# Sending each token to its own expert alone in a two-layer fp32 transformer kernel

## The chip, the cores and the metric

The kernel runs on one core of a Trainium2 chip. The metric is the time on the device in microseconds (us), as the median of three runs. A core has five engines that run side by side, each through its own instructions in order: PE multiplies matrices (PEld loads its stationary operand), DVE is the vector engine, ACT the engine of activation functions, POOL a general-purpose engine, and SP issues transfers. DMA queues carry data between the main memory and the on-chip memories (SBUF; PSUM, into which PE writes).

## The reference

2048 tokens (two sequences of 1024) of width 128 pass four blocks, all in fp32: a retention layer with eight heads, a causal latent attention with 16 heads of width 8, a mixture of experts, and a full attention with 16 heads; a projection with ternary weights ends it. Layer norms stand between. The change touches the mixture of experts:

```python
def moe(x, gate_w, gate_b, W1, b1, W2, b2):
    logits = x @ gate_w.T + gate_b
    top = jnp.argmax(logits, axis=-1)
    onehot = jax.nn.one_hot(top, N_EXPERTS, dtype=x.dtype)       # N_EXPERTS = 4
    h = jax.nn.relu(jnp.einsum('btd,ehd->bteh', x, W1) + b1)     # W1: 4 x 512 x 128
    y = jnp.einsum('bteh,edh->bted', h, W2) + b2                 # W2: 4 x 128 x 512
    return jnp.einsum('bted,bte->btd', y, onehot)
...
x = x + mla_attention(rmsnorm(x, norm1_w), ...)
x = x + moe(rmsnorm(x, norm2_w), gate_w, gate_b, W1, b1, W2, b2)
```

Each token uses the output of one expert, that with the largest logit; the reference computes all four and masks three.

## The kernel before

The retention layer comes first and ends at about 290 us. Then both attentions run as one chain of 224 items, through a loop of ticks. An item is one tile of 128 keys by up to 512 queries for a group of four heads. In each tick `chain_tick` issues, for one item, four score matmuls (`sc`) and the maxima of their rows on DVE (`parts`); for the item 11 ticks back four transposed score matmuls (`sct`) and their exponentials on ACT (`es`); for the item 12 back four matmuls with the values (`acc`), which ACT evicts into `part` and POOL adds to `oT`. `part` is one buffer. In the diagonal tiles of the causal attention POOL also zeroes part of `es` (`bar`). After a group's last score its maxima go by PE, ACT and a small DMA on SP's queue (`qT<-m_rows`) into the queries, three ticks or more before `sct` needs them. All matmul outputs take turns in eight PSUM banks (`slot`). The causal attention fills items 0 to 95, the full one 96 to 223; a group of the full one has eight items, the first of which ACT evicts straight into `oT`.

Everything else runs beside this chain, as jobs cut into stages by `yield`. `side_work` runs at the head of a tick; of each of two lists of jobs, heavy and light, it steps the first one whose tick has come, and the number yielded is how many ticks the next stage has to wait. A job that is due is run to its end.

The heavy list holds the four experts jobs, one for each block of 512 tokens (2 sequences x 2 blocks). Such a job projects the attention's output, norms it (`rmsnorm_T`, which leaves the tokens as rows in `xn` and as columns in `xnT`), computes the gate and its one-hot `oh` on DVE, and then has 16 stages, four to an expert: two with two `first` each, two with two `second` each:

```python
for e in range(NE):
    hT = scratch("e_hT", "hT", (P, NF, BT))
    for i in range(0, NF, 2):
        first(e, i, hT)
        first(e, i + 1, hT)
        bias_2(e) if i else None
        yield 1
    for i in range(0, NC, 2):
        second(e, i, hT)
        second(e, i + 1, hT)
        yield 1
```

`first` is one matmul over 512 tokens (`ph`) and a relu on DVE or ACT; `second` is four accumulating matmuls with 128 tokens (`pmoe`), which DVE multiplies by `oh` and adds to `moe_acc`. `bias_2` adds the second bias on POOL. Then come the layer norm's moments and its application. The weights of all experts are loaded once, by two transfers of 1 MB on SP's queue at tick 12. The jobs' expert stages lie in ticks 37 to 52, 69 to 84, 94 to 109 and 119 to 134.

Of the kernel before, what the change touches and what calls it, by code (L numbers as in the profile page):

```python
# [14 lines left out]
P = 128  # L15
# [8 lines left out]
NE, FF = 4, 512  # L24
NF = FF // P
NEG = -1.0e9
NH = NG * GH
# [33 lines left out]
def block_kernel(  # L61
# [34 lines left out]
    for e in range(NE):  # L96
        nc.gpsimd.memset(rank[:, e : e + 1], float(NE - e))

    def dims(j):
# [58 lines left out]
    def slot(name):  # L158
        return banks[0](name)
# [23 lines left out]
    def transposed(src, name):  # L183

        tp = slot(name)
        for c in range(NC):
            nc.tensor.transpose(tp[:, c * P : (c + 1) * P], src[:, c, :], ident)  # L187
        return tp
# [23 lines left out]
    def scratch(tag, name, shape=(P, NC, P)):  # L212
        return scratch_of[0].tile(list(shape), F32, tag=tag, name=name)

    def rmsnorm_T(src, weight, got, lane=""):
# [9 lines left out]
        yield 2  # L225
        tp = transposed(xn, "xn_ps")
        got["xnT"] = scratch(lane + "xnT", "xnT", (P, BT))
        nc.scalar.activation(got["xnT"], tp, AF.Identity, scale=weight)
# [675 lines left out]
    late = ctx.enter_context(tc.tile_pool(name="late", bufs=1, reuse_waits="tile"))  # L904
    for i, name in enumerate(("w1", "w2")):
        at, n = M_W[name]
        mw[name] = late.tile([P, n], F32, name=f"m_{name}")

    def load_experts():
        for name in ("w1", "w2"):  # L910
            at, n = M_W[name]
            nc.sync.dma_start(out=mw[name], in_=m_w[:, at : at + n])

# [12 lines left out]
    def project(src, w, name, got, tag):  # L926
# [5 lines left out]
        got["py"] = by_tile(oT, w, f"{name}_ps")  # L932

    def experts(b, k):

        got = {}
# [4 lines left out]
        yield from rmsnorm_T(xa, col("norm2"), got, "e_")  # L941
        xnT = got["xnT"]
        pg = by_tile(xnT, mw["gate"], "pgate")
# [17 lines left out]
        nc.gpsimd.tensor_tensor(acc, x1[b][k], xa, ALU.add)  # L961
        yield 1

        def first(e, f, hT):
            ph = slot("ph")
            at = e * FF + f * P
            mm(ph, mw["w1"][:, at : at + P], xnT)
            bias = col("b1", e * NF + f)
            if f % 2:
                nc.vector.tensor_scalar(hT[:, f, :], ph, bias, 0.0, ALU.add, ALU.max)  # L970
            else:
                nc.scalar.activation(hT[:, f, :], ph, AF.Relu, bias=bias)

        def second(e, c, hT):
            py = slot("pmoe")
            for f in range(NF):
                at = (e * NF + f) * P
                mm(
                    py[:, :P], hT[:, f, c * P : (c + 1) * P], mw["w2"][:, at : at + P],
                    start=f == 0, stop=f == NF - 1,  # L980
                )
            nc.vector.scalar_tensor_tensor(  # L982
                acc[:, c, :], py[:, :P], oh[:, c, e : e + 1], acc[:, c, :], ALU.mult, ALU.add
            )

# [7 lines left out]

        for e in range(NE):
            hT = scratch("e_hT", "hT", (P, NF, BT))
            for i in range(0, NF, 2):
                first(e, i, hT)
                first(e, i + 1, hT)
                bias_2(e) if i else None
                yield 1  # L1000
            for i in range(0, NC, 2):
                second(e, i, hT)
                second(e, i + 1, hT)
                yield 1
        mv, r = stats(tiles(acc))
# [76 lines left out]
    def setup():  # L1082
        load_experts()
        yield from ternary()

    class Job:
# [3 lines left out]
        def step(self, tick):  # L1090
            try:
                self.at = max(self.at, tick) + next(self.stages)
            except StopIteration:
                self.done = True


    light = [
# [4 lines left out]
    ]  # L1102
    heavy = []
    for b in range(B):
# [161 lines left out]
```

## Time and profile before

| | us |
|---|---|
| median of three runs | 1192.27 (1191.64 to 1195.5) |
| the profiled execution's own time | 1191.54 |
| its span, first to last instruction | 1189.8 |
| PE busy / share of the span | 1102.6 / 93% |
| DVE busy / share | 825.9 / 69% |
| ACT busy / share | 710.4 / 60% |
| POOL busy / share | 479.8 / 40% |
| granted TensorE clock, mean | 0.975 |

Times below are from the one profiled execution. A group of the page is one line's instructions of one kind on one engine, with how often, how long in all and how long each; behind the bar stands the idle time of the engine before them and what ended it. An fp32 matmul shows as two PE records. The chain is followed back from the last instruction to what released each step, so its shares name what set the end. A line of a stretch gives the busy us of each engine in it, then the granted clock, the DMA share and GB/s. Line 82 is the helper that issues most matmuls, so tiles tell them apart.

### The profile page before, as it was taken

What the parts mean: (1) busy time and instruction counts of PE and PEld (TensorE: products, weight loads), DVE (VectorE), ACT (ScalarE), POOL (GpSimd) and SP (SyncE); (2) the same over time, 40 slices, a digit from 0 to 9 for tenths busy, and PEclk for the clock granted to TensorE, in tenths of its full rate; (3) what the DMA queues carried; (4) which work ended last, traced back from release to release, by engine and by line L of the source; (5) the groups of instructions that cost most, each with busy time, mean ns of one, the idle gap of its engine ahead of it and who ended that gap; (6) DMA issues with size and microseconds to landing.
All of it is one profiled execution on the core that took longest, in us unless ns stands there. A gap on an engine that the chain in (4) does not pass through costs nothing.

```text
span 1189.8 us, 22189 instructions
## 1 busy us (share of the span) xinstructions
PE 1102.6 (93%) x8554; PEld 604.3 (51%) x8554; DVE 825.9 (69%) x1822; ACT 710.4 (60%) x1439; POOL 479.8 (40%) x491
## 2 busy tenths in 40 slices
PE   6999999979889999999999999999989989998993
PEld 5888888755444554554444444444333333333322
DVE  4666766757766667676666677667788888888812
ACT  2465544432666556655565557556768867886891
POOL 4466445411656434443353334423333333323342
PEclk9999999986999999999999999999999999999996
DMA  5511112101000000100010001000100000000000
GB/s 187 164 37 45 41 41 45 28 10 73 10 11 19 1 2 1 21 3 1 2 19 1 1 4 18 2 1 1 19 10 2 1 2 10 1 2 10 1 1 9
DMA packets 14840, 25.56 MB, mean 21 GB/s; under 512 B 2960, under 2 KB 8400, under 8 KB 14352
## 3 DMA queue, kind: packets, MB, share of 16 engines
q1 hardware_dynamic: 14080, 22.30, 7.7%
q8 instruction: 67, 1.10, 0.4%
q0 software_dynamic: 224, 1.05, 0.2%
q10 hardware_dynamic: 432, 0.81, 0.2%
q14 instruction: 37, 0.30, 0.1%
HBM read 10.13 MB, written 1.05 MB: 9 GB/s over the span
## 4 chain that ended last, share of the span: by engine, by line
PE 72%; DVE 17%; POOL 4%; issue 3%; ACT 2%; DMA 1%; SPq 0%; POOLq 0%; DVEq 0%; ACTq 0%
PE sc L82 17%; PE acc L82 15%; PE sct L82 12%; PE pmoe L82 5%; PE ph L82 5%; DVE parts L353 5%; DVE spare L348 2%; PE py L82 2%; PE pv L82 2%; PE pr L82 2%; PE pout L714 1%; PE o_ps L187 1%; PE pg L82 1%; DVE x L205 1%; ACT es L397 1%
## 5 line engine op out<-in xcount | busy, mean ns | idle before, releaser
L397 ACT ACTIVATE es<-sct 128x512 f32<-128x512 f32 (+3 forms) x896 | 426.9, 558 | 218.6 <-PE sct L82 169.0
L353 DVE TENSOR_REDUCE parts<-sc 128x1 f32<-128x512 f32 x640 | 396.9, 682 | 94.4 <-PE sct L82 69.0
L82 PE MATMUL sc<-kT,qT 32*128 32x512 f32 (+3 forms) x1792 | 428.4, 584 | 5.5 <-DVE parts L348 2.7
L82 PE MATMUL sct<-qT,kT 32*128 32x512 f32 (+3 forms) x1792 | 410.6, 578 | 1.4 <-DMA qT<-m_rows 1.1
L423 POOL TENSOR_TENSOR oT<-oT,part 128x512 f32<-128x512 f32 (+3 forms) x192 | 217.5, 1133 | 392.3 <-ACT part L422 388.0
L82 PE MATMUL acc<-es,v_aug 128*32 128x512 f32 (+3 forms) x1792 | 221.6, 558 | 40.6 <-DVE parts L353 29.0
L82 PEld LDWEIGHTS sc<-kT,qT 32*128 32x128 f32 x1792 | 171.7, 189 | 145.2 <-DVE parts L353 73.9
L82 PEld LDWEIGHTS sct<-qT,kT 32*128 32x128 f32 x1792 | 179.1, 184 | 46.0 <-issue 23.3
L348 DVE CUSTOM_DVE_ANT_0 spare<-sc,causal 128x512 f32<-128x512 f32 (+3 forms) x256 | 125.4, 490 | 48.2 <-PE sc L82 12.8
L82 PEld LDWEIGHTS acc<-es,v_aug 128*32 128x32 f32 x1792 | 37.8, 108 | 196.0 <-DVE parts L353 112.5
L422 ACT COPY part<-acc 128x512 f32<-128x512 f32 (+3 forms) x192 | 105.7, 550 | 42.4 <-PE acc L82 36.3
L405 POOL TENSOR_SCALAR_AFFINE_SELECT es<-es 128x512 f32<-128x512 f32 x64 | 40.8, 637 | 118.5 <-ACT es L397 118.5
L771 ACT ACTIVATE og<-pt,cols_sb 128x128 f32<-128x128 f32 x128 | 46.5, 468 | 53.1 <-PE pt L763 53.1
L82 PEld LDWEIGHTS pmoe<-m_w,hT 128*128 128x128 f32 x512 | 59.6, 192 | 16.2 <-DVE parts L353 8.8
L82 PE MATMUL pmoe<-m_w,hT 128*128 128x128 f32 x512 | 65.0, 280 | 0.6 <-DVE parts L348 0.2
L82 PE MATMUL ph<-xnT,m_w 128*128 128x512 f32 x128 | 62.4, 610 | 0.0
L118 POOL TENSOR_TENSOR rstd<-rstd,nhalf 128x4 f32<-128x4 f32 (+1 forms) x44 | 54.7, 1244 | 3.6
L970 DVE TENSOR_SCALAR hT<-ph,cols_sb 128x512 f32<-128x512 f32 x32 | 24.0, 750 | 35.2 <-PE ph L82 35.2
L645 POOL TENSOR_TENSOR swap<-swap,r_cs 128x1024 f32<-128x1024 f32 x16 | 38.7, 2417 | 20.7 <-DMA swap<-plain 20.7
L982 DVE SCALAR_TENSOR_TENSOR moe_acc<-pmoe,oh,moe_acc 128x128 f32<-128x128 f32 x64 | 22.4, 350 | 35.2 <-PE pmoe L82 34.8
L668 ACT COPY v<-pv 128x1024 f32<-128x1024 f32 x16 | 16.2, 1012 | 43.8 <-PE pv L82 43.8
L82 PEld LDWEIGHTS ph<-xnT,m_w 128*128 128x128 f32 x128 | 21.7, 189 | 31.0 <-issue 11.0
(178 smaller groups left out, 1190.1 us busy)
## 6 DMA issues: line engine op xcount, KB each, us to landing
swap<-plain SPq DMA_DIRECT2D x64, 128.0 KB
qT<-dense SPq DMA_DIRECT2D x32, 64.0 KB
kT<-dense SPq DMA_DIRECT2D x32, 64.0 KB
m_w<-in_m_w SPq DMA_DIRECT2D x2, 1024.0 KB
x<-in_x SPq DMA_DIRECT2D x4, 256.0 KB
mcs<-in_m_const SPq DMA_DIRECT2D x4, 256.0 KB
out<-ob SPq DMA_DIRECT2D x4, 256.0 KB
r_rest<-in_r_const POOLq DMA_DIRECT2D x1, 774.0 KB, 7.4
```

The source lines that it names most:

```text
L82: nc.tensor.matmul(o, lhsT, rhs, start=start, stop=stop)
L118: nc.gpsimd.tensor_tensor(r, r, nhalf[:, :n], ALU.pow)
L348: nc.vector.tensor_tensor_reduce(out=spare[:, :n], in0=sc[:, :n], in1=causal[:, BT - n :], scale=1.0, scalar=-3.0e38, op0=ALU.add, op1=ALU ...
L353: nc.vector.tensor_reduce(part, sc[:, :n], AX.X, ALU.max)
L397: nc.scalar.activation(es[n_item][:, j, :n], sct[:, :n], AF.Exp, scale=scale)
L405: nc.gpsimd.affine_select(out=d, in_=d, pattern=[[0, GH], [1, P]], compare_op=ALU.is_ge, fill=0.0, base=0, channel_multiplier=-1,)
L422: nc.scalar.copy(part[:, lo:], acc[:, lo:])
L423: nc.gpsimd.tensor_tensor(sums[i][:, lo:], sums[i][:, lo:], part[:, lo:], ALU.add)
L645: nc.gpsimd.tensor_tensor(swap[n], swap[n], table(n, 1), ALU.mult)
L771: nc.scalar.activation(og[:, a, g, :], pt[a][:, g, :], AF.Identity, bias=col("gn_b", h), scale=col("gn_w", h))
L970: nc.vector.tensor_scalar(hT[:, f, :], ph, bias, 0.0, ALU.add, ALU.max)
L982: nc.vector.scalar_tensor_tensor(acc[:, c, :], py[:, :P], oh[:, c, e : e + 1], acc[:, c, :], ALU.mult, ALU.add)
```

## The change

A job no longer sends its 512 tokens through all four experts. `places` ranks the tokens of each expert: two matmuls with the one-hot (against a triangle of ones and against ones) count the tokens ahead of each token within its tile of 128 and in all, and a chain of small DVE instructions turns this into a row number for each token (`row_of`), such that each expert's tokens begin at a multiple of 128. Four tiles' worth of tokens then fill at most seven tiles (`NT`), and DVE also works out each tile's expert (`expert_of`) and first bias (`bias_1`). Four indirect DMAs from POOL's queue scatter the normed rows into `by_expert` in DRAM, one DMA reads the seven tiles back, PE transposes them, and each tile goes through both matmuls of its own expert. The weights of a tile, 512 KB, are loaded on SP's queue from an address in a register, which is read from `expert_of`; there are three buffers. The results are written to `from_expert` in DRAM, and four indirect DMAs gather them in the tokens' order; one DVE addition puts them into `moe_acc`. A job `clear` fills `by_expert` with zeros at tick 12. The places stages lie in ticks 37, 69, 96 and 123, the eight tile stages in 43 to 50, 75 to 82, 102 to 109 and 129 to 136, the gathers in 53, 85, 112 and 139. The loads of all weights at tick 12 are gone.

```diff
+NT = NC + NE - 1
...
+    ahead = const.tile([P, P], F32, name="ahead")
+    nc.gpsimd.memset(ahead, 1.0)
...
+    count = const.tile([P, NT], F32, name="count")
+    for i in range(NT):
+        nc.gpsimd.memset(count[:, i : i + 1], float(i + 1))
...
-    def load_experts():
-        for name in ("w1", "w2"):
-            at, n = M_W[name]
-            nc.sync.dma_start(out=mw[name], in_=m_w[:, at : at + n])
...
+    def places(oh):
...
+        ps = slot("places")
+        flat_oh = oh.rearrange("p c e -> p (c e)")
+        mm(ps[:, : NC * NE], ahead, flat_oh)
+        mm(ps[:, NC * NE : 2 * NC * NE], ones, flat_oh)
+        got = tiny([2, NC, NE], "counts")
+        nc.vector.tensor_copy(
+            got.rearrange("p a c e -> p (a c e)"), ps[:, : 2 * NC * NE]
+        )
+        rank_, total = got[:, 0], got[:, 1]
+        for c in range(1, NC):
+            nc.vector.tensor_tensor(total[:, c], total[:, c], total[:, c - 1], ALU.add)
+        nc.vector.tensor_tensor(rank_[:, 1:], rank_[:, 1:], total[:, : NC - 1], ALU.add)
...
+        row_of = tiny([NC], "row_of", mybir.dt.uint32)
+        nc.vector.tensor_copy(row_of, where)
...
+        expert_of = tiny([NT], "expert_of", mybir.dt.int32)
+        nc.vector.tensor_scalar(expert_of, nth, -1.0, None, ALU.add)
...
+        return row_of, expert_of, bias_1
...
+        row_of, expert_of, bias_1 = places(oh)
+
+        def indirect(c):
+            return bass.IndirectOffsetOnAxis(ap=row_of[:, c : c + 1], axis=0)
+
+        for c in range(NC):
+            nc.gpsimd.indirect_dma_start(
+                out=by_expert, out_offset=indirect(c), in_=xn[:, c, :], in_offset=None
+            )
+        weights = {}
+
+        def load(i):
+            e = nc.sync.value_load(expert_of[0:1, i : i + 1], min_val=0, max_val=NE - 1)
+            weights[i] = jobs_sb.tile([P, 2, FF], F32, tag="e_w", name="e_w", bufs=3)
+            for a, name in enumerate(("w1", "w2")):
+                nc.sync.dma_start(
+                    out=weights[i][:, a, :], in_=m_w[:, bass.ds(e * FF + M_W[name][0], FF)]
+                )
+
+        for i in range(2):
+            load(i)
+        yield 2
+        rows_in = scratch("e_rows", "e_in", (P, NT, P))
+        nc.sync.dma_start(out=rows_in, in_=by_expert.rearrange("(i p) d -> p i d", p=P))
+        yield 3
+        xgT = scratch("e_cols", "xgT", (P, NT, P))
+        for at in range(0, NT, NC):
+            tp = slot("xg_ps")
+            n = min(NC, NT - at)
+            for i in range(n):
+                nc.tensor.transpose(tp[:, i * P : (i + 1) * P], rows_in[:, at + i, :], ident)
...
+        yield 1
...
+        def first(i):
             ph = slot("ph")
...
+            for f in range(NF):
+                mm(ph[:, f * P : (f + 1) * P], weights[i][:, 0, f * P : (f + 1) * P], xgT[:, i, :])
...
+            return hT
+
+        def second(i, hT):
             py = slot("pmoe")
             for f in range(NF):
...
+                    py[:, :P], hT[:, f, :], weights[i][:, 1, f * P : (f + 1) * P],
                     start=f == 0, stop=f == NF - 1,
                 )
...
+            nc.scalar.copy(rows_out[:, i, :], py[:, :P])
...
+        last = None
+        for i in range(NT + 1):
+            hT = first(i) if i < NT else None
+            if i:
+                second(i - 1, last)
+            last = hT
+            if i + 2 < NT:
+                load(i + 2)
+            if 0 < i <= NE:
+                bias_2(i - 1)
+            yield 1
+        nc.sync.dma_start(out=from_expert.rearrange("(i p) d -> p i d", p=P), in_=rows_out)
+        yield 2
+        made = scratch("e_xn", "e_made")
+        for c in range(NC):
+            nc.gpsimd.indirect_dma_start(
+                out=made[:, c, :], out_offset=None, in_=from_expert, in_offset=indirect(c)
+            )
+        yield 2
+        nc.vector.tensor_tensor(flat(acc), flat(acc), flat(made), ALU.add)
         mv, r = stats(tiles(acc))
...
+    heavy = [Job(12, ends(0, 0, 0), clear())]
```

## The prediction

> **What bounds the kernel now.** I read the page first (busy shares, chain, groups), then stretches of 30 us, then the chain and the timeline inside the stretches where the experts run.
>
> ```profile
> span 1189.8 us, 22189 instructions
> PE 1102.6 (93%) x8554; PEld 604.3 (51%) x8554; DVE 825.9 (69%) x1822; ACT 710.4 (60%) x1439; POOL 479.8 (40%) x491
> ...
> PE sc L82 17%; PE acc L82 15%; PE sct L82 12%; PE pmoe L82 5%; PE ph L82 5%; DVE parts L353 5%; DVE spare L348 2%; PE py L82 2%; PE pv L82 2%; PE pr L82 2%; PE pout L714 1%; PE o_ps L187 1%; PE pg L82 1%; DVE x L205 1%; ACT es L397 1%
> ...
> L82 PE MATMUL pmoe<-m_w,hT 128*128 128x128 f32 x512 | 65.0, 280 | 0.6 <-DVE parts L348 0.2
> L82 PE MATMUL ph<-xnT,m_w 128*128 128x512 f32 x128 | 62.4, 610 | 0.0
> ```
>
> The expert matmuls (ph and pmoe) carry 5% + 5% of the chain that ended last, 119 us of 1189.8. One fp32 matmul is two records.
>
> ```profile
> 750.00:780.00 30.00, 30.00 (x218) 14.24 (x217) 19.78 (x35) 17.42 (x34) 11.45 (x10) 1.00 0.01 1
> 900.00:930.00 30.00, 30.00 (x241) 11.37 (x237) 24.52 (x42) 25.02 (x50) 10.26 (x9) 1.00 0.01 2
> ```
>
> Columns: PE, PEld, DVE, ACT, POOL busy, then granted clock. The first stretch has experts beside attention, the second attention alone. A tick of attention has 24 PE records (8 sc, 8 sct, 8 acc), so the second holds ten ticks of 3.0 us, with DVE at 2.45 and ACT at 2.5 per tick. In the first, DVE and ACT have ten of thirty us free: there the experts' matmuls lengthen the tick, and PE alone is the bound. The chain shows by how much:
>
> ```profile
> 772.62 0.99 PE acc L82 x8
> 773.61 1.98 PE pmoe L82 x16
> ...
> 777.52 1.00 PE acc L82 x8
> ...
> 782.82 1.00 PE acc L82 x8
> 783.82 1.91 PE ph L82 x4
> ```
>
> From acc to acc it is 4.9 us instead of 3.0: what a stage adds on PE is added to the time.
>
> **Part 1, the matmuls.** A job (512 tokens; four jobs) has 16 stages: eight of two ph matmuls of 512 columns, eight of eight pmoe matmuls of 128. By the chain 8 x 1.91 + 8 x 1.98 = 31.1 us, by its shares 119/4 = 29.7; I take 30. The new job has seven tiles, each four ph and four pmoe matmuls of 128 columns, 16 records: 7 x 1.98 = 13.9 us, in stages as long as the pmoe stages were, but eight of them (the first and last half full). Gain 16.1 a job, **64.5 us**. On ACT and DVE a tile has two relus each of 128 columns and one eviction, about as much as the two relus or two accumulations of a stage before, under a PE stage of 4.9 us: nothing. bias_2 moves, its count stays. If PE were not the bound in a tile, DVE's 0.35 us per 128-column PSUM instruction (the accumulations' 350 ns) would show.
>
> **Part 2, new on PE.** Seven transposes: four take 0.66 us in the timeline (o_ps), so 7 x 0.165 = 1.2 us a job, **4.6 us**. The two ranking matmuls (16 columns) lie under DVE's wait below.
>
> **Part 3, ranking and scatter.** `places` puts 19 dependent small instructions on DVE at the head of a tick, before that tick's maxima. The nearest rows are those of the one-hot:
>
> ```profile
> 740.13 0.17 DVE L945 TENSOR_TENSOR lg<-pgate,rowb 128x16 f32<-128x16 f32 x1 [0.21 <-PE pgate L82]
> 740.34 0.17 DVE L954 TENSOR_REDUCE top<-lg 128x4 f32<-128x16 f32 x1
> ...
> 740.85 1.26 POOL L961 TENSOR_TENSOR moe_acc<-x,xa 128x512 f32<-128x512 f32 x1
> 740.96 1.19 DVE L956 TENSOR_TENSOR oh<-oh,rank 128x16 f32<-128x16 f32 x1
> ...
> 743.22 1.07 PE L82 MATMUL acc<-es,v_aug 128*32 128x512 f32 x8 [1.20 <-DVE parts L353]
> ```
>
> They follow each other at 0.205 us, except that one with two SBUF inputs took 1.19 us while POOL ran a 1.26 us instruction; and PE then sat idle 1.20 us for the late maxima. So row_of, the 13th, is ready 0.3 (wait for PE) + 13 x 0.205 + 0.6 (half a POOL instruction) = 3.6 us into the tick, and DVE is through at 4.8.
>
> POOL meanwhile stands at the first scatter; behind it waits the addition of this tick's `part`, which has one buffer, and for that buffer waits ACT's next eviction, in front of the next exponentials. In the instruction order of the changed kernel each later scatter also waits for the one before it to land, all four writing by_expert. An indirect DMA is not in the trace. Near rows:
>
> ```profile
> 2.47 0.97 POOL L513 DMA_DIRECT2D r_cs<-in_r_const  x1
> ...
> 9.62 5.09 SPq L632 DMA_DIRECT2D swap<-plain  x8
> ...
> 14.16 3.25 POOL L645 TENSOR_TENSOR swap<-swap,r_cs 128x1024 f32<-128x1024 f32 x1 [10.15 <-DMA swap<-plain]
> ```
>
> A direct DMA costs POOL 0.57 to 0.97 us of issue; four of the eight swaps are issued by 12.16 (0.636 each) and have landed at 14.16, so 2.0 us for landing. I take 1.0 + 2.0 = 3.0 us a round trip: POOL is free at 3.6 + 3 x 3.0 + 1.0 = 13.6, its addition ends at 14.9 (1.27), ACT's next eviction at 15.5, where 2 x 3.0 = 6.0 is usual: 9.5 late, less 1.0 that PE does ahead into its eight PSUM banks: 8.5 us. In the fourth job (tick 123) the next product is a step's first, which ACT copies straight into oT; that leaves a tick more, 5.5 us. Sum 3 x 8.5 + 5.5 = **31 us**. DVE's own 4.8 us lie under this; with POOL free at once they would cost some 4.4 a job, 17.6 us, which is the lower end; 4.5 us a round trip gives 13 a job, 49 us in all.
>
> The Trainium skill (DMA: Bandwidth & Descriptors, Anatomy of one DMA, SWDGE path) states 2.0 us plus bytes/436e3 per us for a POOL-issued DMA, 2.15 us for 64 KB. An estimate with it: 5.6 us a job, 20 us, and a total 11 us lower. I keep the rows, as they measure issue apart from landing, and I expect 128 row addresses to be no cheaper to issue than a direct DMA.
>
> **Part 4, the clock.** Waiting so long, PE runs empty.
>
> ```profile
> 236.00:240.00 4.00, 4.00 (x50) 3.88 (x47) 1.50 (x3) 2.23 (x7) 0.00 (x0) 1.00 0.02 4
> 240.00:244.00 4.00, 2.56 (x19) 2.25 (x18) 2.35 (x2) 2.84 (x7) 0.07 (x1) 0.93 0.00 0
> 244.00:248.00 4.00, 4.00 (x20) 2.53 (x19) 1.26 (x4) 0.00 (x0) 2.92 (x3) 0.64 0.00 0
> ```
>
> 1.4 us without PE work in four cost clock: (0.07 + 0.36) x 4 / 0.5 = 3.4 us at half. But gaps of 1.2 to 1.45 us later, as the 1.20 above, did not. The skill (TensorE: Matmul & The Clock Gate, What's actually happening) lets the gate close after a whole idle window of 3.4 us on a free-running grid; a gap of 3 to 5 us seldom holds one, so by the rule about nothing, by the row one window at half clock per job after the stall, 1.7 us of lost PE time, **6.8 us**. I take the row.
>
> **Part 5, gather.** Four gathers wait only for the write of from_expert, issued about three ticks before. Behind POOL's addition (1.3) they issue until 5.3, the next addition ends at 6.6 where ACT wants the buffer at 5.4, and the last lands near 7.3, DVE's addition being due at about 6. I take 1.3 us of stall and 1.1 for the addition (DVE's 128x512 SBUF addition is 1089 ns, before the maxima): 2.4 a job, **9.6 us**; at 0.57 us an issue 1.1 us, at 2 us 6.3 us.
>
> **Part 6, the queues.** SP: 28 register reads and 56 weight loads of 256 KB in place of two of 1 MB. A tile's load is asked for once the tile three back is through on PE, 2.0 us into its stage, for use two stages of 4.9 us on: 7.8 us for a register read, two issues (0.4 each by m_w's 398 ns) and a landing of 2 to 3. Hidden. SP's wait for expert_of (4.0 us) holds up the shift rows (qT<-m_rows), which have three ticks. Clearing by_expert is hidden at tick 12 (POOL 40% busy). At the start r_cs leaves POOL behind a dozen more memsets, 0.7 us later: between 0 and 0.7, **0.5 us**. Removing the two big loads gives nothing; no wait names them.
>
> **Sum** against the profiled execution, 1191.5 us (span 1189.8, median of runs 0.7 higher): -64.5 + 4.6 + 31 + 6.8 + 9.6 + 0.5 = -12.0, so 1179.5, and 1180 against the median 1192.27.
>
> **Rivals.**
> - *The waits mostly vanish* (0.2). Scatters return in about 2.2 us, no clock is lost, gathers hide: -64.5 + 4.6 + 20 + 5 + 0.5 = -34: 1158. For it: the page's figure, and DVE and ACT with ten us in thirty free among the experts. Against: POOL's chain has one buffer.
> - *The serial scatters eat it all* (0.17). It takes 12 us more, 3 us a job, 1.0 us in each of a job's three round trips: from 4.0 us on the sign turns. At 5.0 us the four jobs lose 14.5 x 3 + 11.5 = 55 us instead of 31: 1204, slower. For it: an unknown instruction, whose issue on POOL may be 2 us or more; against: 2.0 us landings.
> - *The clock stays down* (0.1). At 268 to 291 it was half for over 20 us. 10 us lost in each of four jobs, 40 instead of 6.8: 1213, slower. Against: with full attention ticks it stayed at 1.00 from 292 to 1168.
> - *Weights come late* (0.06). A register read and address on SP of over 3 us more each holds every tile: 2 us x 20 tiles, 1220.
>
> **Chances.** The forecast, 1170 to 1190, has 0.42; 0.05 goes to mixtures about no change. 0.3%, 3.6 us, is about what a measurement of this kernel tells from no change. Faster 0.62 (the first rival and most of the forecast), same 0.12 (the mixtures and 0.07 of the scatters near their turning point), slower 0.26 (0.10 of the scatters, clock, weights). The range takes in the first rival and the serial scatters: 1158 to 1208; the forecast's own is 1170 to 1190.
>
> **What would show it.** Right: ph and pmoe with 224 records each (4 x 7 x 8) where they had 128 and 512, 64 pmoe accumulations gone, PE busy down by some 60; a stall of 8 to 10 us at each scatter with ACT's `part` eviction waiting for POOL, the four DMA issues some 3 us apart; tiles at 4.9 us from acc to acc; a clock row under 1.00 behind each scatter. Wrong: PE waiting for DMA e_w or SP (late weights); scatters under 2.5 us or over 4 us apart; a clock under 1.00 for over 10 us; tiles above 5.5 us.

## The result, and the profile after

| | before | changed kernel |
|---|---|---|
| median (7 runs each) | 1194.91 us (1191.64 to 1195.81) | 1187.7 us (1185.37 to 1189.37) |
| profiled execution (span) | 1191.54 us (1189.8) | 1185.93 us (1184.2) |
| mean granted clock in it | 0.975 | 0.951 |

The ratio over all runs is 0.995, with a 95% interval of 0.9937 to 0.9963: faster, by 0.5%. The forecast was 1180 us, a gain of 12 us from one profile to the other; the profiles show 5.6 us, the medians 7.2. The sign was right and the time lies in the forecast's range of 1170 to 1190. The gain is about half of what the sum gave. Executions of one kernel differ by some 4 us, so differences of that size between single profiles say little.

From the page of the changed kernel: the span, the busy times, the chain of waits by line; then three lines of the groups.

```profile
span 1184.2 us, 22389 instructions
...
PE 1070.1 (90%) x8406; PEld 594.1 (50%) x8406; DVE 819.4 (69%) x1862; ACT 721.3 (61%) x1499; POOL 513.0 (43%) x541
...
PE sc L83 16%; PE acc L83 14%; PE sct L83 12%; DVE parts L373 4%; DMA by_expert<-xn,row_of 3%; PE ph L83 2%; DVE spare L368 2%; PE pmoe L83 2%; PE py L83 2%; PE pv L83 2%; PE pr L83 2%; PE pout L734 2%; PE o_ps L206 1%; PE pg L83 1%; ACT es L417 1%
```

```profile
L83 PE MATMUL ph<-xgT,e_w 128*128 128x128 f32 x224 | 31.6, 284 | 0.1
...
L83 PE MATMUL pmoe<-e_w,hT 128*128 128x128 f32 x224 | 30.0, 277 | 0.0
...
L1060 POOL DMA_INDIRECT by_expert<-xn,row_of x16 | 16.0, 1000 | 39.8 <-DMA by_expert<-xn,row_of 24.2 <-DVE begun L997 9.2 <-DVE nth L1002 6.4
```

The 640 records of ph and pmoe have become 448, and the two kinds together fall from 10% of the chain to 4%. But PE is busy only 32.5 us less than before, though 65.8 us of expert matmuls went and about 4.6 of transposes came, which would make 61.2. Of the missing 28.7 us, 8.0 are missing in e1_tiles too (below), where the clock does not fall in the loop; the rest goes with the clock, which was at half for 47.8 us there (half of that, 23.9 us, is the most it can add to PE's busy time, by estimate). And a new link stands in the chain, the landing of the scatters, with 3%: POOL waited 24.2 us for it, in 12 waits.

The tiles run as forecast. The chain inside two tiles of the fourth job:

```profile
797.14 1.00 PE acc L83 x8
798.14 1.09 PE ph L83 x8
799.23 0.89 PE pmoe L83 x8
...
802.05 1.00 PE acc L83 x8
```

From acc to acc it is 4.91 us, of which 1.98 are the tile: the 4.9 and 1.98 of the prediction.

The scatter of the first job on POOL:

```profile
391.90 1.15 POOL L1060 DMA_INDIRECT by_expert<-xn,row_of  x1 [6.44 <-DVE nth L1002]
394.59 0.99 POOL L1060 DMA_INDIRECT by_expert<-xn,row_of  x1 [1.54 <-DMA by_expert<-xn,row_of]
398.27 0.96 POOL L1060 DMA_INDIRECT by_expert<-xn,row_of  x1 [2.69 <-DMA by_expert<-xn,row_of]
400.80 0.96 POOL L1060 DMA_INDIRECT by_expert<-xn,row_of  x1 [1.56 <-DMA by_expert<-xn,row_of]
401.77 1.27 POOL L443 TENSOR_TENSOR oT<-oT,part 128x512 f32<-128x512 f32 x1
```

The round trips are 2.69, 3.68 and 2.53 us, 2.97 in the mean: the 3.0 of the prediction, not the 2.15 that it worked out from the Trainium skill (DMA: Bandwidth & Descriptors, Anatomy of one DMA, SWDGE path). From issue to landing alone the 16 scatters took 2.3 us in the median, near the page's figure. POOL turns to its addition 9.9 us after the first issue.

To place the time, I take ACT's eviction of each product (part or oT from acc) as the end of a tick; there are 224 of them, from tick 12 to 235, in every kernel, in the same order. The clock column is the time at half clock between 300 and 1100 us, from the clock's record in the trace.

| kernel | end of tick 36 against before | end of tick 235 against before | from tick 36 to 235 | at half clock |
|---|---|---|---|---|
| before, second profile | +0.8 | +5.2 | +4.3 | 10.2 us |
| changed kernel | +3.0 | -5.4 | -8.4 | 47.8 us |
| changed, second profile | +4.3 | +0.1 | -4.1 | 64.8 us |
| e1_tiles | +1.0 | -53.6 | -54.7 | 0 |
| e2_spread | +3.8 | -20.3 | -24.1 | 37.5 us |
| e3_four | +4.6 | -21.6 | -26.2 | 27.2 us |
| e4_filler | +3.6 | -2.9 | -6.5 | 23.8 us |
| e5_part | +1.4 | -8.8 | -10.2 | 47.7 us |
| e6_split | +1.0 | -29.6 | -30.6 | 13.6 us |
| e7_all | +0.3 | -26.2 | -26.5 | 23.8 us |
| e8_mid | +3.8 | -25.1 | -28.9 | 23.8 us |
| e9_pool | +3.4 | -32.1 | -35.6 | 23.8 us |

Each row is one execution; those of e5_part and e6_split are the fastest of their kernel's six, 3.5 and 4.5 us under its median. Ticks 12 to 36 take the same time in all, to 0.6 us; what differs there was won or lost at the start. The change's own work in the loop lies behind tick 36.

### The profile page after: what moved, and what is told of

Its sections match the earlier page's. It is cut to its first block, busy times and chain, and to the rows that moved or that the text cites. A ratio compares the mean times of both kernels' runs of the same rounds, so it can differ in the third digit from the quotient of the medians.

```text
span 1184.2 us, 22389 instructions
## 1 busy us (share of the span) xinstructions
PE 1070.1 (90%) x8406; PEld 594.1 (50%) x8406; DVE 819.4 (69%) x1862; ACT 721.3 (61%) x1499; POOL 513.0 (43%) x541
## 4 chain that ended last, share of the span: by engine, by line
PE 66%; DVE 17%; POOL 6%; issue 4%; DMA 4%; ACT 2%; SPq 0%; POOLq 0%; DVEq 0%; ACTq 0%
PE sc L83 16%; PE acc L83 14%; PE sct L83 12%; DVE parts L373 4%; DMA by_expert<-xn,row_of 3%; PE ph L83 2%; DVE spare L368 2%; PE pmoe L83 2%; PE py L83 2%; PE pv L83 2%; PE pr L83 2%; PE pout L734 2%; PE o_ps L206 1%; PE pg L83 1%; ACT es L417 1%
## 5 line engine op out<-in xcount | busy, mean ns | idle before, releaser
L83 PE MATMUL sc<-kT,qT 32*128 32x512 f32 (+3 forms) x1792 | 442.3, 599 | 4.8 <-DVE on L768 2.5
L83 PE MATMUL sct<-qT,kT 32*128 32x512 f32 (+3 forms) x1792 | 428.2, 591 | 5.0 <-ACT part L442 4.7
L83 PE MATMUL acc<-es,v_aug 128*32 128x512 f32 (+3 forms) x1792 | 227.3, 572 | 64.8 <-DVE parts L373 36.6
L83 PEld LDWEIGHTS sc<-kT,qT 32*128 32x128 f32 x1792 | 178.9, 195 | 140.0 <-DVE parts L373 74.3
L425 POOL TENSOR_SCALAR_AFFINE_SELECT es<-es 128x512 f32<-128x512 f32 x64 | 40.6, 635 | 93.1 <-ACT es L417 93.1
L1101 DVE TENSOR_SCALAR hT<-ph,bias 128x128 f32<-128x128 f32 x56 | 19.7, 351 | 36.8 <-ACT hT L1103 36.8
L688 ACT COPY v<-pv 128x1024 f32<-128x1024 f32 x16 | 16.2, 1012 | 44.5 <-PE pv L83 44.5
L83 PE MATMUL py<-r_wo,og 128*128 128x128 f32 x256 | 35.2, 296 | 4.0 <-DVE og L867 2.5
L83 PE MATMUL pv<-r_wv,xT 128*128 128x512 f32 x64 | 32.2, 628 | 5.8 <-issue 5.0
L83 PEld LDWEIGHTS py<-r_wo,og 128*128 128x128 f32 x256 | 33.1, 209 | 6.5 <-DVE og L891 1.6
L671 POOL TENSOR_TENSOR qd<-qk,r_rest 128x512 f32<-128x512 f32 x16 | 20.4, 1272 | 36.6 <-DVE qk L668 33.8
L1103 ACT ACTIVATE hT<-ph,bias 128x128 f32<-128x128 f32 x56 | 20.6, 367 | 24.9 <-PE ph L83 13.2
```

The lines of the kernel that those rows point to most:

```text
L83: nc.tensor.matmul(o, lhsT, rhs, start=start, stop=stop)
L425: nc.gpsimd.affine_select(out=d, in_=d, pattern=[[0, GH], [1, P]], compare_op=ALU.is_ge, fill=0.0, base=0, channel_multiplier=-1,)
L1103: nc.scalar.activation(hT[:, f, :], part, AF.Relu, bias=bias_f)
```

## The experiments

**The tiles alone (e1_tiles).** Edit:

```diff
-        row_of, expert_of, bias_1 = places(oh)
...
-        for c in range(NC):
-            nc.gpsimd.indirect_dma_start(
-                out=by_expert, out_offset=indirect(c), in_=xn[:, c, :], in_offset=None
-            )
...
-            e = nc.sync.value_load(expert_of[0:1, i : i + 1], min_val=0, max_val=NE - 1)
+            e = i % NE
...
-                nc.tensor.transpose(tp[:, i * P : (i + 1) * P], rows_in[:, at + i, :], ident)
+                nc.tensor.transpose(tp[:, i * P : (i + 1) * P], xn[:, (at + i) % NC, :], ident)
...
-        nc.vector.tensor_tensor(flat(acc), flat(acc), flat(made), ALU.add)
+        nc.vector.tensor_tensor(flat(acc), flat(acc), flat(rows_out[:, :NC, :]), ALU.add)
```

> The tiles alone: no ranking of tokens, no scatter, no gather, no buffers in DRAM and no clear of them. Each job runs its seven tiles on rows of xn as they stand (tile i takes token block i mod 4 and the weights of expert i mod 4, still loaded for every tile), and the results of four tiles are added to moe_acc; so the output is not the reference's. My theory (the matmuls give what the sum says, and the routing takes most of it back): -64.5 + 4.6 + 4 x 1.1 for the additions and about 2 to 3 for the start = some -53 against before, about 1140 us, ratio to before 0.953 to 0.958, so some 48 us under the changed kernel; the granted clock stays at 1.00 between 400 and 1160 us. Rival A (the matmuls gave less than 64.5, since a tile costs more than the PE stage says): 1155 us or more. Rival B (the start and the placement of buffers cost more than 0.5 us): the first 300 us are 3 us or more later than before here too, although no scatter has run.

Measured: 1137.65 us, ratio 0.9538 (0.9513 to 0.9562). Page:

```profile
span 1135.9 us, 21972 instructions
...
PE 1049.4 (92%) x8390; PEld 583.7 (51%) x8390; DVE 804.5 (71%) x1786; ACT 721.1 (63%) x1499; POOL 481.1 (42%) x508
```

The clock does not fall between 300 and 1100 us, and from tick 36 on the kernel gains 54.7 us. The prediction's -64.5 + 4.6 leaves 5.2 for four additions, 1.3 a job against the 1.1 that I took. (Against the second profile of before it would be 59.0 us instead of 54.7.) So the tiles gave what the sum said, and the shortfall lies in ranking, scatter, gather and the start. Rival A is out; rival B is out for this run, whose start lost only 1.0 us.

With this kernel as the measure the rest can be read tick by tick, since both have the same stages in the same ticks. What the changed kernel takes more in the eight ticks from each ranking on (36 to 44, 68 to 76, 94 to 102, 122 to 130): 10.2, 11.6, 12.4 and 6.8 us, **41.0 us**. In all the other ticks from 36 on: **5.2 us**, nearly all of it where the gathers are: 0.2, 0.4, 2.3 and 2.2 us in the four jobs.

**One scatter in each tick (e2_spread), and four targets (e3_four).** Edits:

```diff
-        for c in range(NC):
-            nc.gpsimd.indirect_dma_start(
...
         for i in range(2):
             load(i)
+        for c in range(NC):
+            yield 1
+            nc.gpsimd.indirect_dma_start(
+                out=by_expert, out_offset=indirect(c), in_=xn[:, c, :], in_offset=None
+            )
```

```diff
+    targets = [*others, by_expert]
...
-                out=by_expert, out_offset=indirect(c), in_=xn[:, c, :], in_offset=None
+                out=targets[c], out_offset=indirect(c), in_=xn[:, c, :], in_offset=None
```

> The same work, with the four scatters of a job one in each of four ticks instead of all in one. Theory (the round trips of the four scatters hold POOL, and behind it the one buffer of part, ACT and PE): POOL no longer waits for a landing at the scatters (24.2 us in 12 waits in the changed kernel); of some 41 us that the ticks of ranking and scattering took beyond plain ticks, about 4.4 us a job stay for the burst of small instructions on DVE; gain 13 to 20 us, about 1170 us, ratio to before 0.98. The half-clock time between 400 and 770 us falls from 47.8 us to under 15 us. Rival (DVE's burst and the clock that falls behind it are the cost, the scatters only lie beside them): gain under 5 us, 1183 us or more.

> The four scatters stay in one tick, but each writes a DRAM buffer of its own, so none waits for the one before it; only the last one's buffer is read back, so three quarters of the tokens are left out of the experts and the output is not the reference's. This takes away the wait for a landing and leaves the four issues (0.95 us each) and DVE's burst. Theory (the wait for landing is the cost): the four issues follow each other at about 1 us instead of 3, POOL is free some 5.5 us earlier in each job, gain 4 x 4 to 5.5 = 14 to 22 us, about 1168 to 1174 us. Rival (DVE's burst and the clock): under 5 us. Against the kernel with spread scatters it says what the issues themselves cost: 3 x 0.95 us a job at most, 11 us.

Measured: 1173.35 us (0.9824, 0.9802 to 0.9846) with the scatters spread; 1170.67 us (0.9805, 0.9781 to 0.9828) with four targets. POOL in the first job with four targets:

```profile
393.54 1.16 POOL L1061 DMA_INDIRECT other<-xn,row_of  x1 [6.44 <-DVE nth L1003]
395.00 0.98 POOL L1061 DMA_INDIRECT other<-xn,row_of  x1 [0.30 <-issue]
396.29 0.96 POOL L1061 DMA_INDIRECT other<-xn,row_of  x1 [0.30 <-issue]
397.55 0.96 POOL L1061 DMA_INDIRECT by_expert<-xn,row_of  x1 [0.30 <-issue]
398.54 1.29 POOL L443 TENSOR_TENSOR oT<-oT,part 128x512 f32<-128x512 f32 x1
```

The issues follow each other at 1.3 us and POOL is free 5.0 us after the first, instead of 9.9. In the four stretches the cost falls from 41.0 to 21.0 us (4.0, 5.6, 5.7, 5.7). So the waits for a landing, with the clock that they cost, are worth 20.0 us; the other half of the price is there without them. The issues themselves cost nothing that shows: with the scatters spread, the time from tick 36 on is 2.1 us longer than with four targets, not shorter. The half-clock time is not what I expected with spread scatters: 37.5 us, not under 15.

**PE kept at work (e4_filler).** Edit:

```diff
+        def busy():
+            fill = slot("fill")
+            for _ in range(4):
+                mm(fill, ident, causal)
+
+        busy()
...
-        yield 2
+        yield 1
+        busy()
+        yield 1
```

> The changed kernel with eight matmuls more per job, whose result nobody reads: four of 512 columns in PE's queue at the ranking, four a tick later, so that PE has work in the stall. The theory that the lost clock is a cost of its own: the half-clock time after 400 us falls by over 10 us and the kernel gains 3 to 8 us, about 1181 us. Theory of the round trips alone (PE's stall is what costs, and the clock behind it little): the matmuls fill idle time and nothing changes, 1185 to 1190 us; if they fall behind the stall instead of into it, 8 x 0.5 = 4 us a job are added, up to 16 us.

Measured: 1186.98 us, ratio 0.9942 (0.992 to 0.9964), no different from the changed kernel. Granted clock in the stretch behind the first scatter, in the changed kernel (columns: PE, PEld, DVE, ACT, POOL busy, then the clock):

```profile
392.00:396.00 4.00, 2.59 (x21) 1.22 (x24) 3.46 (x15) 0.83 (x2) 2.04 (x2) 1.00 0.46 145
...
400.00:404.00 4.00, 0.28 (x1) 0.28 (x2) 0.48 (x3) 0.92 (x2) 2.49 (x3) 0.72 0.05 16
404.00:408.00 4.00, 4.00 (x14) 0.83 (x17) 0.00 (x0) 1.97 (x5) 1.64 (x2) 0.50 0.38 115
```

and with the filler:

```profile
400.00:404.00 4.00, 3.69 (x32) 1.18 (x24) 2.96 (x17) 2.11 (x5) 2.33 (x3) 1.00 0.10 33
404.00:408.00 4.00, 3.41 (x14) 0.96 (x18) 0.11 (x1) 2.94 (x6) 1.90 (x2) 0.73 0.39 115
```

The half-clock time is halved, 47.8 to 23.8 us, and the four stretches cost 39.9 instead of 41.0 us. The filler is 7.8 us of PE work a job (its 64 records keep PE busy for 31.1 us), and in the fourth job, where the stall is shortest, it added 0.8 us. So this does not part the clock's price from the filler's own; it only shows that filling PE does not pay here.

**A second buffer for part (e5_part).** Edit:

```diff
-            part = pools["work"].tile([P, BT], F32, tag="part", name="part", bufs=1)
+            part = pools["work"].tile([P, BT], F32, tag="part", name="part", bufs=2)
```

> The changed kernel with two buffers for part instead of one; all else stays, four scatters in one tick, each waiting for the one before it to land. The claim of the prediction is that the one buffer carries POOL's stall to ACT and PE. If so, ACT can evict one product more while POOL stands: up to a plain tick of 3.0 us less per job at the scatters, and the 1.3 us at the gathers, so 6 to 14 us faster than the changed kernel, 1174 to 1182 us. Rival: ACT and PE are held by DVE's burst or by POOL's masks of es just as long; then less than 3 us, 1185 us or more.

Measured: 1186.07 us, ratio 0.9927 (0.9903 to 0.9951); by the table 1.8 us less than the changed kernel from tick 36 on. Its rival holds. The four stretches cost 5.5, 11.1, 14.5 and 6.8 us: the first job gains 4.8 us, the second 0.4, the fourth nothing, the third loses 2.1 (its stretch has 23.9 us at half clock, 17.1 in the changed kernel). What PE waits for says why. First job (388 to 412 us) of the changed kernel, and then its second (512 to 535 us):

```profile
PE sct L83 <- ACT part L442: 4.2, 1, 4.2
```

```profile
PE acc L83 <- POOL es L425: 5.0, 1, 5.0
PE acc L83 <- DVE parts L368: 4.1, 2, 2.8
```

And POOL in the second job with two buffers:

```profile
525.10 0.96 POOL L1060 DMA_INDIRECT by_expert<-xn,row_of  x1 [1.57 <-DMA by_expert<-xn,row_of]
526.08 0.64 POOL L425 TENSOR_SCALAR_AFFINE_SELECT es<-es 128x512 f32<-128x512 f32 x1
```

In the second and third job the ticks under the scatter are on the diagonal of causal attention. There POOL masks es (L425) before PE may multiply, and that mask stood behind the last scatter; in the second job with two buffers PE's acc still waited 5.4 us for it. The prediction named the addition and part's buffer as what is queued behind the scatters; the mask it overlooked.

**The ranking in pieces (e6_split), and everything spread (e7_all).** Edits, the second on top of the first. `places` ends its tick before `some` and before `at`; `tiles_of` holds begun to expert_of, a yield, and which to bias_1; `fill_constants` stands behind the load of r_rest and fills what was filled ahead of both loads.

```diff
-        row_of, expert_of, bias_1 = places(oh)
+        put = {}
+        yield from places(oh, put)
...
+        ranking = tiles_of(put)
+        for c in range(NC):
...
+            if c in (1, 2):
+                next(ranking)
```

```diff
+            if c % 2:
+                yield 1
-        yield 2
         nc.vector.tensor_tensor(flat(acc), flat(acc), flat(made), ALU.add)
+        yield 1
         mv, r = stats(tiles(acc))
...
+        fill_constants()
```

> The kernel with spread scatters, and now the ranking's 19 instructions on DVE cut into five pieces of two to five instructions (0.4 to 1.1 us each, places and scatters in six ticks as before, no tick more). Theory (DVE's burst of 3.6 us in one tick is what is left of the ranking's cost, 20.9 us over four jobs in the kernel with four targets): a plain tick has 0.5 us of DVE free, so most of it goes under the ticks: 12 to 18 us faster than the kernel with spread scatters, 1155 to 1161 us, ratio to before 0.967 to 0.973. Rival (the cost is DVE's total work, not its burst, or the two ranking matmuls and the clock): under 5 us, 1168 us or more. The half-clock time after 400 us (37.5 us with spread scatters) falls below 15 us if the burst makes the gaps on PE.

> The kernel with the split ranking, and in addition the gathers two in each of two ticks, DVE's addition of e_made a tick before the statistics instead of in their tick, and the constants of the ranking filled on POOL after the two loads of r_const instead of before. Theory: gathers and additions cost some 10 us in the changed kernel (5.2 us more than in the kernel of tiles alone, which has the additions but no gathers, and some 5 for the additions); half of it goes, 4 to 7 us; the start is 0.9 us earlier (r_cs at 2.5 us and ACT's first plain at 8.6 us as before the change). So 5 to 8 us faster than the kernel with the split ranking, some 1150 us. Rival: the addition and the gathers are hidden already and only the order changes: under 2 us.

Measured: 1166.69 us (0.9764, 0.9741 to 0.9787) and 1166.67 us (0.9762, 0.9735 to 0.9788). The split gave 6.5 us from tick 36 on, not 12 to 18, and the half-clock time fell to 13.6 us. That 13.6 us is of e6_split's fastest run: its mean clock was 0.969, that of the other five 0.958 to 0.963, so most runs had more of it. The medians say the same of the gain, 6.7 us. By the eight or nine ticks of each ranking it gave 0.3, 4.1, 0.7 and 1.8 us, most in the second job, where in e2_spread the clock had been at half for 13.7 us. Spreading the gathers gave nothing (the medians agree to 0.02 us; the 4.1 us more from tick 36 on are against that fastest run): its rival holds. The constants behind the two loads brought the start of r_cs back from 3.05 to 2.5 us; tick 36 ends 0.65 us earlier than in e6_split.

**The pieces in the middle of the tick (e8_mid).** Edit, with the constants filled late:

```diff
                 maxima(s_items[si], got_s)
+            while mid:
+                mid.pop(0)()
             if ti is not None:
                 exps(ti, got_t)
...
-        yield from places(oh, put)
+        ranking = places(oh, put)
+        next(ranking)
+        for _ in range(2):
+            mid.append(lambda: next(ranking))
+            yield 1
```

> The kernel with the split ranking, with its pieces placed behind the first two of a tick's four maxima instead of at the tick's head; the first scatter follows its piece, and the constants are filled after the two loads of r_const as in the kernel before this one (0.65 us of start by the traces). At the head each piece met POOL's addition of part: counts x3 took 1.65 us instead of 0.56, prior 1.09 instead of 0.17, begun 0.98 instead of 0.18, picked 1.47 instead of 0.34, 3.9 us a job. Theory (DVE's small instructions with two SBUF inputs wait while POOL runs a 128x512 addition, and this is why the split gave 7 us instead of 12 to 18): in the middle of the tick POOL has finished, the pieces fall to their 0.17 to 0.56 us, and the kernel gains 4 to 9 us more, 1157 to 1162 us, ratio 0.970 to 0.973. Rival (the pieces cost because DVE has no room in these ticks, wherever they stand): under 2 us, 1165 us or more.

Measured: 1166.71 us, ratio 0.9759 (0.9737 to 0.9782): no gain. The fourth job in e6_split, two pieces on DVE:

```profile
761.26 1.65 DVE L972 TENSOR_TENSOR counts<-counts 128x4 f32<-128x4 f32 x3
...
776.86 1.47 DVE L1025 TENSOR_TENSOR picked<-which,cols_sb 128x112 f32<-128x112 f32 x1
```

with POOL beside them:

```profile
761.24 1.27 POOL L443 TENSOR_TENSOR oT<-oT,part 128x512 f32<-128x512 f32 x1 [2.95 <-ACT part L442]
...
776.86 1.26 POOL L443 TENSOR_TENSOR oT<-oT,part 128x512 f32<-128x512 f32 x1 [1.82 <-ACT part L442]
```

The same pieces in e8_mid:

```profile
768.11 0.55 DVE L980 TENSOR_TENSOR counts<-counts 128x4 f32<-128x4 f32 x3
...
783.22 0.36 DVE L1033 TENSOR_TENSOR picked<-which,cols_sb 128x112 f32<-128x112 f32 x1
```

The mechanism holds for the instructions: away from POOL's addition the instructions are short again, the ranking's DVE time falls from 24.0 to 16.2 us over the four jobs. The price was wrong: the ranking's ticks take 118.1 us in all, 117.5 in e6_split. The rival's number came out (under 2 us); its reason, that DVE has no room in these ticks, fits but is not shown, since DVE's work in them did fall and what used up the gain was not traced.

**Sums and products on POOL (e9_pool).** Edit, on the kernel with the split and the late constants:

```diff
+        add, mul = ALU.add, ALU.mult
+        pool = nc.gpsimd.tensor_tensor
         for c in range(1, NC):
-            nc.vector.tensor_tensor(total[:, c], total[:, c], total[:, c - 1], ALU.add)
+            pool(total[:, c], total[:, c], total[:, c - 1], add)
...
-        nc.vector.tensor_reduce(used, some, AX.X, ALU.add)
+        pool(pair, some[:, :, :2], some[:, :, 2:], add)
+        pool(used, pair[:, :, 0], pair[:, :, 1], add)
```

> Spread scatters, and the ranking's sums and products on POOL: 19 additions and products of at most 112 columns there, six instructions (a copy, the comparisons and the two conversions, 1.05 us a job) left on DVE; seven ticks in place of six, one tick less for the landing of e_in. The constants are filled late. The middle-of-tick kernel has shown that the ranking's instructions cost about the same time after they had become 7.8 us shorter on DVE. Theory (in these ticks DVE's maxima fill the tick, so 3.7 us of ranking per job lengthen them wherever they stand, while POOL has 1.7 us of 3.0 free): 2.7 us a job leave DVE, 6 to 11 us in all from the first job to the last, about 1156 to 1161 us. Rival (a small instruction on POOL costs about 1.2 us, as rstd's 128x4 does, so 19 of them are 23 us a job, three times what POOL has free, and ACT's part waits again): slower than 1175 us.

Measured: 1159.99 us (1158.35 to 1161.08), ratio 0.9706 (0.9689 to 0.9723). POOL in the fourth job:

```profile
767.15 0.20 POOL L988 TENSOR_TENSOR pair<-some 128x8 f32<-128x8 f32 x1
767.43 0.20 POOL L990 TENSOR_TENSOR used<-pair 128x4 f32<-128x4 f32 x1
767.71 0.21 POOL L992 TENSOR_TENSOR prior<-earlier,used 128x16 f32<-128x16 f32 x1
```

A small instruction costs POOL 0.20 us, not the 1.2 of the rival. From tick 36 on this is 4.9 us faster than e6_split and 6.7 faster than e8_mid, which has the same half-clock time; the ranking's ticks take 113.1 us. This is the low end of the theory, and it is the fastest kernel of the study that does all of the work: 3% under before, some 28 us under the changed kernel.

**Both kernels once more (e10_before, e11_after).** No edit.

> The kernel before once more, unchanged, for a second profile of it. In ten profiles of changed kernels the first attention tick (oT evicted from acc) came 0.4 to 5.2 us later than in the one profile of before, with a half-clock stretch near 14 us that is 3.4 to 10.2 us long. Theory (about 1 us of this is the change, 0.65 of it the memsets ahead of r_cs, and the rest is drawn anew in every execution): this profile starts r_cs at 2.47 us and ACT's first plain at 8.6 us again, but its first attention tick may lie anywhere from 0 to 4 us after the other's 293.5 us. Rival (the change itself delays the start by 3 us): it lies within 0.3 us of it.

> The changed kernel once more, unchanged, for a second profile. Theory (the start is drawn anew, the rest of the program repeats itself): the first attention tick comes 0.8 to 5 us later than 293.5 us, not at 297.07 again, but from tick 36 to the last the time is within 1 us of the first profile's, and the four jobs' ranking and scatter cost 41 us over plain ticks within 1 us. Rival (the stalls themselves vary from run to run): the jobs differ by over 1 us each.

Measured, one run each: 1197.03 and 1191.89 us. The start: before's second profile is 0.8 us later at tick 36 than its first, the changed kernel's 1.3 later than its own first. So the start differs from one execution of a kernel to the next, as in the theory. The eleven profiles of changed kernels lie at +0.3 to +4.6 us; two of before are too few to say whether it spreads as far. The rest did not repeat as well as I expected. The ranking costs 11.8, 12.0, 12.2 and 6.7 us, 42.7 in all (41.0 before), the first job 1.5 us more; in sum 4.3 us more from tick 36 on, with 17 us more at half clock. And before lost 4.3 us in one place, with no scatter in it:

```profile
616.00:620.00 4.00, 2.89 (x22) 0.80 (x20) 3.92 (x8) 1.26 (x5) 3.75 (x6) 0.98 0.29 32
620.00:624.00 4.00, 3.83 (x16) 1.41 (x20) 0.41 (x2) 1.09 (x2) 0.67 (x1) 0.50 0.00 0
624.00:628.00 4.00, 4.00 (x24) 2.02 (x28) 1.62 (x3) 2.23 (x5) 1.68 (x2) 0.50 0.02 4
```

In this stretch PE paused for 1.1 us in four (first line), and the clock then stayed at half for 10.2 us. The first profile of before pauses at the same place for 1.0 us and keeps its clock, so the pause alone does not settle it:

```profile
615.00:619.00 4.00, 3.04 (x23) 0.80 (x20) 3.92 (x8) 1.26 (x5) 3.73 (x6) 1.00 0.33 35
```

## Why the prediction was half right

The signs of the terms held, and so did the size of the largest. What failed is the size of two costs: ranking, scatter and clock (parts 3 and 4) were put at 37.8 us and took 41.0, because another wait and a longer half clock stood in two of the four jobs; and the start (part 6) was put at 0.5 us and took 3.0. Its own sum, against what the traces give (in us, from one profile to the other):

| step | forecast | measured |
|---|---|---|
| matmuls and transposes (1, 2) | -64.5 + 4.6 = -59.9 | -59.9, taken as forecast: with the additions -54.7 |
| ranking, scatter, clock (3, 4) | 31 + 6.8 = 37.8 | 41.0; second profile 42.7 |
| gather (5), wait | 4 x 1.3 = 5.2 | 5.2; second profile 7.9 |
| gather (5), additions | 4 x 1.1 = 4.4 | 5.2, the rest of the -54.7 |
| start (6) | 0.5 | 3.0; second profile 4.3 |
| sum | -12.0 | -5.5 |

- **Right:** parts 1 and 2, to within a microsecond in fifty-five by these two profiles. Reading a tile's price as its PE time held: ticks with a whole tile took 4.4 to 5.3 us, most of them about 4.9. Right too: the round trip in the mean (3.0 against 2.97), the issue (1.0 against 1.00), SP and the weights (PE never waited for e_w).
- **Right by luck:** the gather's wait. Four equal stalls of 1.3 us were forecast; the same 5.2 us fell almost wholly on the last two jobs (0.2, 0.4, 2.3, 2.2).
- **Mis-sized, the first term:** part 3 with part 4, "8.5 us" a job (5.5 in the fourth) with 1.7 for the clock, 37.8 in all. Measured 41.0. The first and last job are at 10.2 and 6.8, near the forecast (10.2 and 7.2). The second and third are at 11.6 and 12.4, and there the prediction had the wait wrong: the mask of es on POOL stood behind the scatters and held PE's acc for 5.0 and 4.0 us. "for that buffer waits ACT's next eviction" was the carrier in the first job alone; e5_part shows it. In the fourth job PE waited for DVE's maxima. In the second and third stretch the clock was also at half for 17.1 us each, against 6.8 and 3.4 in the first and fourth; how the 1.4 and 2.2 us over the forecast divide between mask and clock stays open.
- **Mis-sized, the second term:** the start, "between 0 and 0.7, 0.5 us". With the memsets ahead of it r_cs starts 0.58 us later, and e7_all, which fills them later, is 0.66 us earlier at tick 36 than e6_split. The rest is not theirs: e8_mid and e9_pool fill them late too, and are 3.8 and 3.4 us late. It goes with the clock. The six profiles with 37.5 to 44.4 us at half clock ahead of 300 us, both of before among them, are 0 to 1.4 us late at tick 36; the seven with 47.8 or 51.2 us, the changed kernel's two among them, 3.0 to 4.6. The prediction put no clock in this term. What holds the clock down there, and whether the change makes it likelier, stays open.
- **The lower end was near:** "with POOL free at once they would cost some 4.4 a job, 17.6 us". With POOL free 5.0 us after the first issue it was 21.0, with 17.1 us of half clock in these stretches. That DVE's burst lies under POOL's stall in the changed kernel is neither shown nor refuted: no run splits the burst and leaves the four scatters in one tick.
- **The clock:** one half-clock window of 3.4 us a job was forecast; between 300 and 1100 us it was 47.8 us, not 13.6. Behind the scatters of the second job:

```profile
522.00:526.00 4.00, 2.76 (x16) 1.22 (x20) 2.92 (x11) 0.48 (x1) 1.70 (x2) 0.50 0.53 153
526.00:530.00 4.00, 1.40 (x16) 1.09 (x16) 2.12 (x10) 0.83 (x4) 0.96 (x1) 0.50 0.48 163
530.00:534.00 4.00, 1.56 (x14) 0.76 (x17) 0.00 (x0) 0.36 (x1) 3.13 (x4) 0.50 0.05 16
```

  PE worked 5.7 of 12 us here, in short bursts, and the clock stayed at half for 17.1 us; the prediction counted one window and not the bursts. The Trainium skill (TensorE: Matmul & The Clock Gate, What's actually happening) has the clock return after a busy window of 3.4 us. That fits this stretch, where the first such window came at its end. It does not fit before's own profile, where PE shows as busy throughout from 272 to 288 us at half clock, and there the measurement decides:

```profile
276.00:280.00 4.00, 4.00 (x13) 2.11 (x15) 3.06 (x16) 0.46 (x2) 0.00 (x0) 0.50 0.01 4
```

  What the half clock costs is not settled: 17 us more of it came with 4.3 us more time in the second profile, 10.2 us with 4.3 in before, while e4_filler took 24 us of it away and gained no time.
- **Its signs:** 224 records each of ph and pmoe, issues about 3 us apart and tiles at 4.9 us came as forecast. "PE busy down by some 60" did not (32.5), and one sign of being wrong appeared, "a clock under 1.00 for over 10 us" (17.1 in the second job).
- **No rival came true.** The serial scatters, with the ranking, took back 41 of 60 us, not all; the turning point of 4.0 us a round trip was not reached in the mean. The waits did not vanish, but e2_spread shows that they can: 2.4 us of POOL's waits for a landing are left of 24.2.

In a sum of -60 and +48, an error of 6.5 us, 14% of the costs, halves the result. The terms of the gain were rows of the trace; most of the costs were built of steps that the trace of before does not show, an indirect DMA above all. A range about the difference is as wide as theirs, and the 10 us to each side that I gave it covered the error.

## What to carry to other kernels

When a step is queued on an engine, list everything that stands behind it there in each phase of the loop, not only in the phase that was looked at: an in-order queue with a rare second client (here the causal masks) has two prices. Spread a chain of dependent transfers over the ticks of the work beside it, one in each; that alone took back 15.7 us of the 46 that the routing cost. And shorter instructions need not make a shorter tick: 7.8 us less on DVE gained nothing, while moving sums and products to POOL, which had room, gained 5 to 7 us.

## What the runs showed of the hardware

An indirect DMA of 128 rows of 512 bytes cost POOL 0.95 to 1.15 us of issue, where the two direct ones at the start cost 0.97 and 0.57. It landed 2.2 to 3.7 us after its issue (median 2.3). In the changed kernel the second scatter of each job was the slow one (3.4 to 3.7 us, the others 2.2 to 2.4), in stretches in which DMA moved 145 to 163 GB/s; whether that delayed it is not shown. A small addition or product on POOL took 0.20 to 0.22 us (4 to 16 columns), where rstd's power over 128x4 took 1.24 and an addition of 512 columns 1.27. And of two profiles of the kernel before, with nearly the same pause of PE (1.1 and 1.0 us in four), the clock fell to half in one, for 10.2 us, and not in the other.
